# Two graph layers on one core: the first four graphs issued from a written-out opening with held loads

## The chip, the core and the metric

The kernel runs on one core of a Trainium2 chip. TensorE (PE) multiplies and transposes, VectorE (DVE), ScalarE (ACT) and GpSimd (POOL) work elementwise, and SyncE (SP) issues most DMAs. Each engine takes its instructions in order; engines wait for one another, and for DMAs, through semaphores. The metric is device time in microseconds of one execution; lower is better.

## The reference

64 graphs of 256 nodes with 256 features, all float32. Layer 0 normalises rows, aggregates over the degree-normalised adjacency and applies a weight. Layer 1 normalises again and combines a 17-tap convolution over the nodes, message passing over distances in a 3-dimensional embedding, and a GRU-like gate.

```
# layer 0
h   = relu(layernorm(x));  A = adj + I;  d = rowsum(A) ** -0.5   (0 where the sum isn't positive)
x   = x + relu((d * A * d) @ h @ W.T + b)
# layer 1
h   = relu(layernorm(x))
c   = relu(bn2(conv17(relu(bn1(conv1(h))))) + h)
s   = h @ w_se.T + b_se;  E = exp(-|s_n - s_m|^2)
m   = E @ relu(h @ w_msg.T + b_msg)
gi  = [c, m] @ w_ih.T + b_ih;  gh = h @ w_hh.T + b_hh
r, z = sigmoid(gi_r + gh_r), sigmoid(gi_z + gh_z)
out = x + (1 - z) * tanh(gi_n + r * gh_n) + z * h
```

## The kernel before, in words

One stage covers layer 0 and the first part of layer 1 for all 64 graphs, a loop over n = 0 to 68 (B + 5 passes). A second stage does the convolution's spectra and products and the gates. Graphs are loaded in pairs (G = 2), and a graph is two blocks of 128 rows (NB = 2). In pass n, PE works on graph n for layer 0 and on graphs n - 2, n - 4 and n - 5 for layer 1.

For each graph, layer 0 is this chain:

- `load` (lines 816 to 826) or, for the first pair, `load_one` (828): x and the adjacency come in.
- DVE takes row moments (`row_moments`, 832) and row sums (`degrees`, 844); POOL raises them to the power -1/2 (`factors`, 862); ACT writes the scaled, normalised rows `hs` (`layer0_in`, 876).
- PE transposes the adjacency (`turn_adj`, 891), ACT copies it out as `adjT`, POOL adds the unit matrix to make `adjH`, which has two buffers.
- PE multiplies (`aggregate`, 910: `ag`), ACT copies out `aggT`, PE multiplies by the weight (`project`, 925: `o`), and DVE makes the new rows x2 and their moments. POOL makes scales, and ACT writes the normalised rows `h2` (`norm`). DVE and ACT also empty PSUM banks; there are five general ones.

Layer 1's first part then turns h2 (`turn_h`, 984: `ht`), and multiplies it for the messages (`messages`, 1032: `ms`) and the 1-tap convolution (`conv1`, 1021: `c`). The weights are turned on PE as well (`turn_part`, `turn_away`), and the parts of w_ih and w_hh are written back turned. The batch-norm vectors go through `small_turns` (PE `t_bn`), `small_norms` (DVE and POOL, up to `sc`, `sh` and the diagonal `dg`), and `small_shift` (PE `t_b1`, which reads `dg`). The tap weights come by `TL` (`taps_load`, 643), a DMA of 2.2 MB issued by POOL, and are scaled by ACT.

The order around the change is written by hand. A `Pinned` wrapper (line 94) makes every instruction of an engine keep its place in the program's order among its engine's others. PE, ACT, DVE and POOL compute through such wrappers, so their lines are all the wrapper's, L102. DMAs issued as `nc.sync.dma_start` or `nc.scalar.dma_start` aren't pinned, and a planner places them. Work that follows PE's is deferred: `after(k, go)` puts it on a list, and every `beat` lowers all counts by one and issues what has fallen below zero. So `after(2, go)` issues at the third beat that follows.

In the kernel before, the first two graphs are loaded one by one and graphs 2 and 3 as a pair. The small vectors are issued by ACT's queue (`small_loads`, 697), and the loop starts at n = 0 with extra steps for n = 0 and n = 1 at the end of a pass.

Of the kernel before, what the change touches and what calls it, by code (L numbers as in the profile page):

```python
# [11 lines left out]
FP = mybir.dt.float32  # L12
# [173 lines left out]
def gnn_kernel(  # L186
# [9 lines left out]
    nc = tc.nc  # L196
# [14 lines left out]
    def scratch(name, shape):  # L211
# [26 lines left out]

    pe, act, vec, pool = (
        Pinned(tc, e) for e in (nc.tensor, nc.scalar, nc.vector, nc.gpsimd)
    )
    due = []
    paced = Paced(pool, vec, act)
# [1 line left out]
    def after(beats, go):  # L247
        due.append([beats, go])
# [296 lines left out]
    with ExitStack() as one:  # L545
# [11 lines left out]
        def beat(us):  # L557
            come_due()
            paced.issue(*(k * us for k in share))
# [36 lines left out]

        def load_part(src, o0, i, tag):
            nat = prep.tile([P, 2, i], FP, tag=f"nat{i}", name=f"nat_{tag}_{o0}", bufs=2)
            nc.sync.dma_start(
                nat, src[o0 * P : (o0 + 2) * P].rearrange("(c p) i -> p c i", p=P)  # L600
            )
            return nat
# [73 lines left out]
        def gate_biases_load():  # L676
            bi = prep.tile([P, 2 * D], FP, tag="bi", name="bi")
            bh = prep.tile([P, 2 * D], FP, tag="bh", name="bh")
            nc.sync.dma_start(bi, b_ih[0 : 2 * D].partition_broadcast(P))
            nc.sync.dma_start(bh, b_hh[0 : 2 * D].partition_broadcast(P))  # L680
            nc.sync.dma_start(bnB[:, 0:D], b_ih[2 * D : 3 * D].partition_broadcast(P))
            nc.sync.dma_start(bnB[:, D:], b_hh[2 * D : 3 * D].partition_broadcast(P))
            nc.sync.dma_start(dft, nc.inline_tensor(dft_table(), name="dft_c").ap())
            hold["b"] = bi, bh

        def gate_biases():
# [7 lines left out]
        ones = prep.tile([P, P], FP, tag="ones", name="ones")  # L694
        dg = prep.tile([P, DC, P], FP, tag="dg", name="dg")

        def small_loads():
            for k, v in enumerate((bn1_g, bn2_g, bn1_b, bn2_b, bn1_m, bn2_m, bn1_v, bn2_v)):
                nc.scalar.dma_start(
                    rows[DC * k : DC * (k + 1), :], v.rearrange("(c p) -> c p", p=P)  # L700
                )
            nc.scalar.dma_start(wsn, w_se)
            nc.scalar.dma_start(bmB[:, 0, 0:D], b_msg.partition_broadcast(P))
            nc.scalar.dma_start(bmB[:, 0, D : D + 3], b_se.partition_broadcast(P))
            nc.gpsimd.memset(ones, 1.0)

        def small_turns():

# [107 lines left out]
        def load(g):  # L816

            xt = io.tile([P, NR, D], FP, tag="x", name=f"x_{g}", bufs=3)
            at = io.tile([P, NR, N], FP, tag="adj", name=f"adj_{g}", bufs=3)
            st[g].update(both=(xt, at))  # L820
            for b in range(G):
                rb = slice(b * NB, (b + 1) * NB)
                st[g + b].update(xt=xt[:, rb, :], at=at[:, rb, :])
            if g > 0:
                nc.sync.dma_start(xt, x[g : g + G].rearrange("b (c p) d -> p (b c) d", p=P))
                nc.sync.dma_start(at, adj[g : g + G].rearrange("b (c p) d -> p (b c) d", p=P))

        def load_one(b):
            nc.sync.dma_start(st[b]["at"], adj[b].rearrange("(c p) d -> p c d", p=P))
            nc.sync.dma_start(st[b]["xt"], x[b].rearrange("(c p) d -> p c d", p=P))  # L830

        def row_moments(g, rows):
            xt, _ = st[g]["both"]
# [7 lines left out]
        def pairs(t):  # L841
            return t.rearrange("p (k r) -> p k r", k=2)

        def degrees(g, rows=range(NR)):

            _, at = st[g]["both"]
            mv = st[g]["mv"]
            if rows[0] == 0:
                for key in ("base", "pn"):
                    st[g][key] = small.tile(  # L850
                        [P, 2 * NR], FP, tag=key, name=f"{key}_{g}", bufs=1
                    )
                st[g]["deg"] = small.tile([P, NR], FP, tag="deg", name=f"deg_{g}", bufs=1)
            rs = slice(rows[0], rows[-1] + 1)
            deg, base, pn = st[g]["deg"][:, rs], pairs(st[g]["base"]), pairs(st[g]["pn"])
            vec.tensor_reduce(deg, at[:, rs, :], AX.X, ALU.add)
            vec.tensor_scalar(base[:, 0, rs], deg, 1.0, TINY, ALU.add, ALU.max)
            vec.tensor_scalar(base[:, 1, rs], mv[:, rs, 1], EPS, None, ALU.add)
            vec.tensor_scalar(pn[:, 0, rs], deg, 1.0, 0.0, ALU.add, ALU.is_gt)
            vec.tensor_scalar(pn[:, 1, rs], mv[:, rs, 0], -1.0, None, ALU.mult)  # L860
# [27 lines left out]
                    bias=nmr[:, r : r + 1], scale=rsd[:, r : r + 1],  # L888
                )

        def turn_adj(g):
            s = st[g]
            t = bank(f"at_{g}").rearrange("p (c i) -> p c i", c=NB)
            for jc in range(NB):
                for ic in range(NB):
                    pe.transpose(
                        t[:, jc, ic * P : (ic + 1) * P], s["at"][:, ic, jc * P : (jc + 1) * P], ident
                    )

            def keep():  # L900
                s["adjT"] = work.tile([P, NB, N], FP, tag="adjT", name=f"adjT_{g}", bufs=6)
                act.copy(s["adjT"], t)

            def hat():
                s["adjH"] = work.tile([P, NB, N], FP, tag="adjH", name=f"adjH_{g}")
                pool.tensor_tensor(s["adjH"], s["adjT"], eye, ALU.add)
            after(1, keep)
            after(2, hat)

        def aggregate(g):  # L910
            s = st[g]
# [205 lines left out]


        load(0)
        load_one(0)  # L1120
        nat_w0 = load_part(w0, 0, D, "w0")
        nc.sync.dma_start(b0B, b0.partition_broadcast(P))
        load_one(1)
        nat_wm = load_part(w_msg, 0, D, "wm")
        small_loads()
        load(G)
        L(WI, 0)()
        L(WI, 2)()

        full = eye.rearrange("p c d -> p (c d)")  # L1130
        t = ps_own.tile([P, NB, 512], FP, tag="ms", name="first_ms")
        for nb in range(NB):
            pe.matmul(t[:, nb, :], ident, full, start=True, stop=True)
        t = ps_own.tile([P, NB, D], FP, tag="c1", name="first_c1")
        pe.matmul(t, ident, full, start=True, stop=True)
        row_moments(0, range(NB))
        degrees(0, range(NB))
        factors(0, range(NB))
        turn_adj(0)
        beat(0.4)  # L1140
        layer0_in(0, range(NB))
        turn_part(w0T, nat_w0, 0, D, "w0")
        nat_w1 = load_part(conv1_w.rearrange("o i k -> o (i k)"), 0, D, "w1")
        row_moments(0, range(NB, NR))
        degrees(0, range(NB, NR))
        beat(0.4)
        factors(0, range(NB, NR))
        after(2, lambda: layer0_in(0, range(NB, NR)))
        after(3, lambda: row_moments(G, range(NR)))

        cv.bank, cv.beat = bank, beat
        items = []
# [35 lines left out]

        FILTER, SPECTRA, PRODUCTS = 2, 7, 4
        filtering = []  # L1190
        for n in range(B + 5):
            even, odd = n % G == 0, n % G == 1
            if filtering and not items:
                filtering.clear()
# [2 lines left out]
                conv_start()  # L1197
            if even and n + 2 * G < B:
                load(n + 2 * G)
            if 2 <= n <= B + 1:  # L1200
                turn_h(n - 2)
            beat(0.4)
            item()
            if n < B:
                aggregate(n)
                if odd and n + 1 < B and n > 0:
                    after(2, lambda n=n: factors(n + 1))
                    for r in range(NR):
                        after((5, 7, 8, 9)[r], lambda r=r, n=n: layer0_in(n + 1, (r,)))
                if even and 0 < n < B - G:  # L1210
                    for r in (0, 2):
                        after(1 + r // 2, lambda r=r, n=n: row_moments(n + G, (r, r + 1)))
                if even and n + G < B:
                    after(4, lambda n=n: degrees(n + G))
            beat(1.7)
            item()
            if even and 4 <= n <= B + 2:
                turn_cols(n - 4)
            beat(0.2)
            if n + 1 < B:  # L1220
# [4 lines left out]
                pass_messages(n - 5)  # L1225
            beat(1.7)
            item(True)
            if 2 <= n <= B + 1:
                messages(n - 2)
            beat(1.7)  # L1230
            item()
            if even and 4 <= n <= B + 2:
                distance(n - 4)
            beat(0.6)
            item()
# [1 line left out]
                project(n)  # L1237
            beat(1.7)
            item(True)
            if 2 <= n <= B:  # L1240
                conv1(n - 2)
            elif n == B + 2:
                conv1(B - 1)
            beat(1.7)
            item()
            if n == 0:
                small_turns()
                turn_part(wmT, nat_wm, 0, D, "wm")
                T(WI, 0)()
                L(WI, 4)()  # L1250
                own_bank("ms", 0, bmB)
            if n == 1:
                small_shift()
                turn_part(w1T, nat_w1, 0, D, "w1", scale=sc[:, 0:DC])
                beat(0.4)
                own_bank("c1", 0, b1B)
                T(WI, 2)()
                L(WH, 0)()
            if n >= 2 and later:
                for go in later.pop(0):  # L1260
                    go()
                if not later:
# [329 lines left out]
```

## Time and profile before

| | |
|---|---|
| Time before, median of 3 | 2079.03 us (2078.04 to 2083.53) |
| The profiled execution's own time | 2078.45 us |
| Its span | 2076.7 us |
| Granted PE clock over the span | 0.997 |
| PE busy in 0 to 10, 10 to 20, 20 to 30 us | 5.26, 8.32, 6.21 us |
| PE busy in 40 to 50 us | 10.00 us |
| DMA moved in 10 to 20, 20 to 30 us | 326, 352 GB/s |

A timeline line gives start, busy time, engine, source line, operation, output and inputs, shape and count. What stands in brackets is the engine's idle time just before, and what ended it. A window line gives busy time and count for PE, PE's weight loads, DVE, ACT and POOL, then the granted clock, the share of the DMA engines' time and GB/s. A matmul in float32 counts as two instructions.

### The profile page before, as it was taken

Reading aid. Unit: us, or ns where it says so; the run is one execution under the profiler, and the core shown is the slowest. Engines: PE = TensorE matmul, PEld = TensorE weight load, DVE = VectorE, ACT = ScalarE, POOL = GpSimd, SP = SyncE. Lnnn points to the kernel's source line nnn. Section 1 sums busy time; section 2 is a strip of 40 time slices with the busy share of each in tenths; the row PEclk is TensorE's granted clock in tenths of the full one; section 3 lists DMA queues with packets and bytes.
Section 4 is the critical chain, followed back from the end, with each engine's and each line's share of the span. In section 5 each row is a group of like instructions: output and inputs, shape, how many; then the busy total and the mean of one; then the engine's idle time right before and its main releaser. Section 6 shows DMA issues by size and latency. Waiting matters only on the chain. (4 is left out here: it accounts for less than half of the span.)

```text
span 2076.7 us, 31189 instructions
## 1 busy us (share of the span) xinstructions
PE 2028.5 (98%) x9977; PEld 1727.0 (83%) x9977; DVE 1404.7 (68%) x3181; ACT 997.5 (48%) x2165; POOL 1108.9 (53%) x1313
## 2 busy tenths in 40 slices
PE   7999999999999999899999999999999999999998
PEld 6877777888888787788888888888888888888887
DVE  6656666544688887337889815989924989965444
ACT  5756666665457676522344532234442234443333
POOL 4343333334775665347667527766726767644433
PEclk9999999999999999999999999999999999999999
DMA  9697987657765554656333455533346424322231
GB/s 307 241 255 245 264 252 251 208 178 228 242 203 195 178 178 148 202 178 203 122 117 117 138 177 187 167 102 117 126 154 195 155 92 127 117 87 89 95 97 61
DMA packets 292456, 352.84 MB, mean 170 GB/s; under 512 B 19491, under 2 KB 232118, under 8 KB 291638
## 3 DMA queue, kind: packets, MB, share of 16 engines
q1 hardware_dynamic: 291680, 346.26, 52.5%
q0 software_dynamic: 288, 4.46, 0.6%
q8 instruction: 80, 1.31, 0.3%
q14 instruction: 82, 0.67, 0.1%
q10 hardware_dynamic: 326, 0.14, 0.0%
HBM read 224.43 MB, written 126.35 MB: 169 GB/s over the span
## 5 line engine op out<-in xcount | busy, mean ns | idle before, releaser
L102 DVE SCALAR_TENSOR_TENSOR Xf<-Xf 128x256 f32<-128x256 f32 (+1 forms) x248 | 185.7, 763 | 6.1 <-ACT Xf L102 5.1
L102 DVE TENSOR_TENSOR Xf<-y,k 128x256 f32<-128x256 f32 x184 | 69.0, 416 | 178.3 <-PE y L102 175.3
L102 PE MATMUL ta<-T,S 128*128 128x256 f32 x768 | 186.6, 379 | 0.0
L102 PE MATMUL y<-wf,Xf 128*128 128x256 f32 x768 | 182.4, 380 | 2.5 <-DVE Xf L102 1.4
L102 POOL TENSOR_TENSOR rz<-u,p 128x256 f32<-128x256 f32 x64 | 48.0, 749 | 244.6 <-ACT u L102 244.6
L102 POOL TENSOR_TENSOR rs<-ve,mhalf 128x2 f32<-128x2 f32 (+1 forms) x65 | 52.2, 803 | 226.8 <-DVE nm L102 221.6
L102 ACT ACTIVATE rz<-rz 128x512 f32<-128x512 f32 x128 | 80.2, 627 | 180.6 <-DVE rz L102 180.6
L102 PEld LDWEIGHTS y<-wf,Xf 128*128 128x128 f32 x768 | 144.0, 190 | 24.9 <-DVE Xf L102 2.6
L102 PEld LDWEIGHTS ta<-T,S 128*128 128x128 f32 x768 | 145.9, 190 | 19.8
L102 PE MATMUL n<-wiT,hx 128*128 128x256 f32 x512 | 152.3, 379 | 0.0
L102 POOL TENSOR_TENSOR xs<-Xf 128x256 f32<-128x256 f32 x92 | 69.9, 766 | 133.9 <-PE y L102 72.7
L102 DVE SCALAR_TENSOR_TENSOR h2l<-rz,h2l 128x256 f32<-128x256 f32 x128 | 102.8, 803 | 53.6 <-POOL h2l L102 53.6
L102 POOL TENSOR_TENSOR aT<-e,adjT 128x512 f32<-128x512 f32 x64 | 85.8, 1358 | 94.1 <-ACT e L102 94.1
L102 PE MATMUL n<-whT,hx 128*128 128x256 f32 x512 | 131.4, 379 | 0.0
L102 PE MATMUL n<-wiT,xcT 128*128 128x256 f32 x512 | 131.4, 379 | 0.0
L102 PE MATMUL o<-w0T,aggT 128*128 128x256 f32 x512 | 125.6, 388 | 5.7 <-ACT aggT L102 4.1
L102 PE MATMUL ag<-adjH,hs 128*128 128x256 f32 x512 | 123.0, 382 | 7.5 <-POOL adjH L102 6.1
L102 PE MATMUL nm<-aT,mso 128*128 128x256 f32 x512 | 123.0, 384 | 7.1 <-POOL aT L102 4.5
L102 PE MATMUL ms<-wmT,h2T 128*128 128x259 f32 x512 | 124.3, 385 | 1.5 <-DVE h2T L102 1.5
L102 POOL TENSOR_TENSOR adjH<-adjT,eye 128x512 f32<-128x512 f32 x64 | 83.6, 1306 | 76.8 <-ACT adjT L102 76.8
L102 PE MATMUL c<-w1T,h2T 128*128 128x256 f32 x512 | 122.8, 383 | 0.0
L102 PEld LDWEIGHTS o<-w0T,aggT 128*128 128x128 f32 x512 | 95.3, 191 | 28.7 <-issue 5.6
(183 smaller groups left out, 5253.1 us busy)
## 6 DMA issues: line engine op xcount, KB each, us to landing
wf<-wfd SPq DMA_DIRECT2D x284, 256.0 KB
wfd<-fo SPq DMA_DIRECT2D x32, 576.0 KB
x2d<-x SPq DMA_DIRECT2D x64, 256.0 KB
h2d<-h SPq DMA_DIRECT2D x64, 256.0 KB
hTd<-h2T SPq DMA_DIRECT2D x64, 256.0 KB
h1d<-c1o SPq DMA_DIRECT2D x64, 256.0 KB
xnd<-xnT SPq DMA_DIRECT2D x64, 256.0 KB
h1l<-h1d SPq DMA_DIRECT2D x64, 256.0 KB
```

What stands on the lines that cost most here:

```text
L102: return self.tc.keep_in_program_order(getattr(self.engine, op)(*args, **kwargs))
```

## The change

A fifth wrapper, `sp`, pins most of SP's loads to the program's order. Graphs 0 to 3 are loaded one by one (`load_one`, adjacency first), with the first weight between graphs 0 and 1. The eleven small loads move from ACT's queue to SP's, behind the first part of w_ih. A one-column `warm` activation stands first on ACT. The warm-up matmuls on PE shrink to three, each on 32 rows. `degrees` takes the row sums ahead of the row moments, and `turn_adj` takes its beats and the engine of the unit-matrix sum as arguments; graph 1's sum goes to DVE. Passes 0 to 3 are replaced by `begin()`, which writes out their steps in another order: layer 0 of the four graphs stands in front, the weight turns and layer 1 of graphs 0 and 1 follow. The loop starts at n = 4.

```diff
-    pe, act, vec, pool = (
-        Pinned(tc, e) for e in (nc.tensor, nc.scalar, nc.vector, nc.gpsimd)
+    pe, act, vec, pool, sp = (
+        Pinned(tc, e) for e in (nc.tensor, nc.scalar, nc.vector, nc.gpsimd, nc.sync)
...
+        nc.gpsimd.memset(ones, 1.0)
+
         def small_loads():
...
-                nc.scalar.dma_start(
+                sp.dma_start(
                     rows[DC * k : DC * (k + 1), :], v.rearrange("(c p) -> c p", p=P)
                 )
...
-            if g > 0:
+            if g > G:
                 nc.sync.dma_start(xt, x[g : g + G].rearrange("b (c p) d -> p (b c) d", p=P))
...
-        def degrees(g, rows=range(NR)):
+        def degrees(g, rows=range(NR), stats=lambda: None):
...
             vec.tensor_reduce(deg, at[:, rs, :], AX.X, ALU.add)
+            stats()
+            mv = st[g]["mv"]
...
-        def turn_adj(g):
+        def turn_adj(g, at=(1, 2), by=pool):
...
-                pool.tensor_tensor(s["adjH"], s["adjT"], eye, ALU.add)
-            after(1, keep)
-            after(2, hat)
+                by.tensor_tensor(s["adjH"], s["adjT"], eye, ALU.add)
+            after(at[0], keep)
+            if at[1] is None:
+                return hat
+            after(at[1], hat)
...
         load(0)
+        load(G)
         load_one(0)
         nat_w0 = load_part(w0, 0, D, "w0")
-        nc.sync.dma_start(b0B, b0.partition_broadcast(P))
-        load_one(1)
+        for b in range(1, 2 * G):
+            load_one(b)
+        sp.dma_start(b0B, b0.partition_broadcast(P))
         nat_wm = load_part(w_msg, 0, D, "wm")
+        L(WI, 0)()
         small_loads()
-        load(G)
-        L(WI, 0)()
+        nat_w1 = load_part(conv1_w.rearrange("o i k -> o (i k)"), 0, D, "w1")
         L(WI, 2)()
 
+        warm = prep.tile([P, 1], FP, tag="warm", name="warm")
+        act.activation(warm, mhalf[:, 0:1], AF.Relu)
+
...
+        own_ms = ps_own.tile([P, NB, 512], FP, tag="ms", name="first_ms")
+        own_c1 = ps_own.tile([P, NB, D], FP, tag="c1", name="first_c1")
+        for r, t in enumerate((own_ms[:, 0, :], own_ms[:, 1, :], own_c1)):
+            at = slice(32 * r, 32 * (r + 1))
+            pe.matmul(t, ident[at, :], full[at, :], start=True, stop=True)
+
+        def stats(b):
+            g, rows = b // G * G, range(b % G * NB, (b % G + 1) * NB)
+            degrees(g, rows, lambda: row_moments(g, rows))
...
+        def begin():
+            stats(0)
+            turn_adj(0, (0, 0))
+            beat(0.4)
+            scale_rows(0)
+            turn_part(w0T, nat_w0, 0, D, "w0")
+            hat = turn_adj(1, (0, None), vec)
+            beat(0.4)
+            stats(1)
+            hat()
+            scale_rows(1)
+            rows_in(0)
+            turn_adj(2, (0, 0))
+            beat(0.4)
+            stats(2)
+            rows_in(1)
+            aggregate(0)
+            beat(1.7)
+            turn_adj(3, (0, 1))
+            scale_rows(2)
+            beat(0.4)
+            stats(3)
+            rows_in(2)
+            turn_part(wmT, nat_wm, 0, D, "wm")
+            aggregate(1)
+            load(2 * G)
+            scale_rows(3)
+            beat(1.7)
+            project(0)
+            beat(1.7)
+            rows_in(3)
+            T(WI, 0)()
+            L(WI, 4)()
+            aggregate(2)
+            beat(1.7)
+            project(1)
+            beat(1.7)
+            small_turns()
+            beat(0.1)
+            aggregate(3)
+            beat(1.7)
+            turn_adj(4)
+            own_bank("ms", 0, bmB)
+            beat(0.4)
+            row_moments(2 * G, range(NR))
+            degrees(2 * G)
+            project(2)
+            beat(1.7)
+            turn_h(0)
+            small_shift()
+            factors(2 * G)
+            beat(0.4)
+            turn_part(w1T, nat_w1, 0, D, "w1", scale=sc[:, 0:DC])
+            own_bank("c1", 0, b1B)
+            load(3 * G)
+            messages(0)
+            beat(1.7)
+            project(3)
+            beat(1.7)
+            conv1(0)
+            beat(1.7)
+            layer0_in(2 * G, range(2))
+            turn_h(1)
+            beat(0.4)
+            T(WI, 2)()
+            L(WH, 0)()
+            for k in range(2):
+                for go in later.pop(0):
+                    go()
+            layer0_in(2 * G, range(2, NR))
+            messages(1)
+            beat(1.7)
+            conv1(1)
+            beat(1.7)
...
-        for n in range(B + 5):
+        begin()
+        for n in range(4, B + 5):
```

The steps for n = 0 and n = 1 and the conditions on small n leave the loop with it.

More of the change, by code (lines that the diff above doesn't have):

```diff
@@ L598, in load_part @@
             nat = prep.tile([P, 2, i], FP, tag=f"nat{i}", name=f"nat_{tag}_{o0}", bufs=2)
-            nc.sync.dma_start(
+            sp.dma_start(
                 nat, src[o0 * P : (o0 + 2) * P].rearrange("(c p) i -> p c i", p=P)
@@ L678, in gate_biases_load @@
             bh = prep.tile([P, 2 * D], FP, tag="bh", name="bh")
[L679 to L683, printed above, removed]
+            sp.dma_start(bi, b_ih[0 : 2 * D].partition_broadcast(P))
+            sp.dma_start(bh, b_hh[0 : 2 * D].partition_broadcast(P))
+            sp.dma_start(bnB[:, 0:D], b_ih[2 * D : 3 * D].partition_broadcast(P))
+            sp.dma_start(bnB[:, D:], b_hh[2 * D : 3 * D].partition_broadcast(P))
+            sp.dma_start(dft, nc.inline_tensor(dft_table(), name="dft_c").ap())
             hold["b"] = bi, bh
@@ L695, in gnn_kernel @@
         dg = prep.tile([P, DC, P], FP, tag="dg", name="dg")
+        nc.gpsimd.memset(ones, 1.0)
         def small_loads():
             for k, v in enumerate((bn1_g, bn2_g, bn1_b, bn2_b, bn1_m, bn2_m, bn1_v, bn2_v)):
-                nc.scalar.dma_start(
+                sp.dma_start(
                     rows[DC * k : DC * (k + 1), :], v.rearrange("(c p) -> c p", p=P)
                 )
[L702 to L705, printed above, removed]
+            sp.dma_start(wsn, w_se)
+            sp.dma_start(bmB[:, 0, 0:D], b_msg.partition_broadcast(P))
+            sp.dma_start(bmB[:, 0, D : D + 3], b_se.partition_broadcast(P))
         def small_turns():
@@ L828, in load_one @@
         def load_one(b):
-            nc.sync.dma_start(st[b]["at"], adj[b].rearrange("(c p) d -> p c d", p=P))
-            nc.sync.dma_start(st[b]["xt"], x[b].rearrange("(c p) d -> p c d", p=P))
+            sp.dma_start(st[b]["at"], adj[b].rearrange("(c p) d -> p c d", p=P))
+            sp.dma_start(st[b]["xt"], x[b].rearrange("(c p) d -> p c d", p=P))
         def row_moments(g, rows):
@@ L842, in pairs @@
             return t.rearrange("p (k r) -> p k r", k=2)
-        def degrees(g, rows=range(NR)):
+        def degrees(g, rows=range(NR), stats=lambda: None):
             _, at = st[g]["both"]
-            mv = st[g]["mv"]
             if rows[0] == 0:
@@ L1130, in gnn_kernel @@
+        act.activation(warm, mhalf[:, 0:1], AF.Relu)
         full = eye.rearrange("p c d -> p (c d)")
[L1131 to L1149, printed above, removed]
+        own_ms = ps_own.tile([P, NB, 512], FP, tag="ms", name="first_ms")
+        own_c1 = ps_own.tile([P, NB, D], FP, tag="c1", name="first_c1")
@@ new lines, in gnn_kernel, with scale_rows, rows_in @@
+        for r, t in enumerate((own_ms[:, 0, :], own_ms[:, 1, :], own_c1)):
[4 more added lines that the diff above has]
+            degrees(g, rows, lambda: row_moments(g, rows))
+        def scale_rows(b):
+            factors(b // G * G, range(b % G * NB, (b % G + 1) * NB))
+        def rows_in(b):
+            layer0_in(b // G * G, range(b % G * NB, (b % G + 1) * NB))
@@ L1199, in gnn_kernel @@
                 load(n + 2 * G)
-            if 2 <= n <= B + 1:
+            if n <= B + 1:
                 turn_h(n - 2)
@@ L1205, in gnn_kernel @@
                 aggregate(n)
-                if odd and n + 1 < B and n > 0:
+                if odd and n + 1 < B:
                     after(2, lambda n=n: factors(n + 1))
@@ L1209, in gnn_kernel @@
                         after((5, 7, 8, 9)[r], lambda r=r, n=n: layer0_in(n + 1, (r,)))
-                if even and 0 < n < B - G:
+                if even and n < B - G:
                     for r in (0, 2):
@@ L1216, in gnn_kernel @@
             item()
-            if even and 4 <= n <= B + 2:
+            if even and n <= B + 2:
                 turn_cols(n - 4)
@@ L1227, in gnn_kernel @@
             item(True)
-            if 2 <= n <= B + 1:
+            if n <= B + 1:
                 messages(n - 2)
@@ L1231, in gnn_kernel @@
             item()
-            if even and 4 <= n <= B + 2:
+            if even and n <= B + 2:
                 distance(n - 4)
@@ L1239, in gnn_kernel @@
             item(True)
-            if 2 <= n <= B:
+            if n <= B:
                 conv1(n - 2)
@@ L1245, in gnn_kernel @@
             item()
[L1246 to L1259, printed above, removed]
+            if later:
                 for go in later.pop(0):
```

## The prediction

> **What bounds the kernel now.** I read the page first (busy shares, 40 slices), then each engine's timeline over the first 75 us, one-microsecond windows there, and SP's waits.
>
> ```profile
> span 2076.7 us, 31189 instructions
> ...
> PE 2028.5 (98%) x9977; PEld 1727.0 (83%) x9977; DVE 1404.7 (68%) x3181; ACT 997.5 (48%) x2165; POOL 1108.9 (53%) x1313
> ...
> PE   7999999999999999899999999999999999999998
> ```
>
> PE is busy 98%, and idles 48 us in all. The change edits the first four graphs, so what it can win is what PE loses in the first slice (the 7). PE's timeline shows those losses and a landmark:
>
> ```profile
> 2.79 3.53 PE L102 MATMUL first_ms<-eye,ident 128*128 128x512 f32 x4 [2.79 <-POOL eye L568]
> ...
> 7.02 0.60 PE L102 MATMUL at<-ident,adj 128*128 128x128 f32 x4
> ...
> 11.38 2.46 PE L102 MATMUL ag<-adjH,hs 128*128 128x256 f32 x8 [3.32 <-POOL adjH L102]
> ...
> 25.38 2.80 PE L102 MATMUL o<-w0T,aggT 128*128 128x256 f32 x8 [3.79 <-ACT aggT L102]
> ...
> 47.97 0.60 PE L102 MATMUL ht<-ident,h 128*128 128x128 f32 x4
> ```
>
> The `ht` at 47.97 is `turn_h(2)`, the first work of n = 4. Before it lies the very set of PE work that `begin()` issues; from n = 4 the program is the same. So the change is worth 47.97 minus the time at which `turn_h(2)` starts afterwards. After each gap the granted clock (third number from the end) is halved:
>
> ```profile
> 13.00:14.00 1.00, 1.00 (x4) 0.71 (x4) 0.00 (x0) 0.62 (x2) 0.27 (x2) 0.50 1.09 378
> 27.00:28.00 1.00, 1.00 (x4) 0.72 (x4) 0.00 (x0) 1.00 (x3) 0.43 (x1) 0.50 1.08 383
> ```
>
> It has a price: from 25.38 to `ht` at 30.64 PE does 1.73 + 4 x 0.44 = 3.5 us of work (spacings of the same groups after 34 us: `o` 1.73, four transposes 0.44) in 5.3, so 1.8 is lost; the first gap likewise about 1.9. DVE, ACT, POOL and SP around it:
>
> ```profile
> 14.51 0.43 DVE L102 BATCH_NORM_STATS2 st<-x 128x6 f32<-128x256 f32 x1 [2.96 <-DMA x<-in_x_dram]
> ...
> 23.39 0.48 DVE L102 TENSOR_SCALAR dg<-ident,sh 128x128 f32<-128x128 f32 x2
> ```
> ```profile
> 7.13 1.28 ACT L102 ACT_TABLE_LOAD   x1 [7.13 <-DMA rows<-in_L_gnn_bn_v_dram]
> ```
> ```profile
> 36.20 0.76 POOL L102 DMA_DIRECT2D w2n<-in_L_gnn_conv_w_dram  x1
> ...
> 45.58 0.62 POOL L102 DMA_DIRECT2D w2n<-in_L_gnn_conv_w_dram  x1
> ```
> ```profile
> SPq L825 <- DMA adj<-in_adj_dram: 2.0, 1, 2.0
> ...
> SPq L829 <- DMA rows<-in_L_gnn_bn_g_dram: 0.9, 1, 0.9
> ```
>
> DVE waited in order for graph 2's rows until 14.51, and the second PE gap hangs on that through moments(0), scales(0) and norm(0), which stands ahead of aggT(1) on ACT. ACT's table came late because eleven small DMAs stood on its queue. SP itself waited for small loads.
>
> **What the skill says.** "TensorE: Matmul & The Clock Gate", Part 1: an idle window of about 3.4 us drops PE to half rate, and sustained work of that length restores it; the 0.50 after gaps of 3.32 and 3.79 agrees. Part 3 of that page: matmuls on different 32-row groups run together; here the four `di` matmuls of K = 5 take 0.71 against 1.89 for four full ones of equal width. "ScalarE: Activation LUTs", What ACT_TABLE_LOAD costs: 1.28 us; the trace has 1.28. "DMA: Bandwidth & Descriptors", Issuing engines are not separate DMA queues: moving an issue to another engine saves only sequencer time; the trace shows 350 to 385 GB/s for 12 to 29 us whoever issued.
>
> **The change part by part** (durations from the trace of before).
>
> *Warm-up.* Three matmuls of 512 columns on three row groups instead of three in sequence. In sequence they end near 7.0; together I take two cold passes of 0.9, so 2.79 + 1.8 + 0.3 = 4.9. PE is then not warm, so at(0) takes 0.9 and not 0.44.
>
> *ACT table and small loads.* The warm activation puts the 1.28 us at about 2 to 3.3; the eleven issues leave ACT. Worth nothing alone: ACT waits for at(0) until 5.9. On SP the small loads add 11 x 0.45 = 5 us after WI 0, until about 12 to 13. `rows` is wanted by t_bn at 22, `bmB` at 24, so hidden; uncovered, they would cost PE their delay one for one.
>
> *Loads.* Nine of 256 KB ahead at 365 GB/s is 0.7 us each: graph 3 complete by about 10 (first x usable at 4.41 before, issued 1.25). Graph 4/5's 1 MB is due by 20; DVE wants it at 26.6, so hidden by 6 us. SP's own order is now held: WI 4 waits there for WI 0's turn (about 19.5), the second w_hh part for t_w1 (about 32), and the stores x2d, hTd and graph 6's load can stand behind them; graph 6 is wanted near 50 and a store has a second buffer, so I cost this at nothing, up to 1 if a store comes late.
>
> *Start.* at(0) 4.9 to 5.9; adjT(0) on ACT 0.57; adjH(0) on POOL 1.27; factors(0), now behind it, 1.88; two hs 1.09; five hand-overs of 0.06: ag(0) at 11.0, against 11.38. So the front end wins 0.4 only: POOL in series replaces PE and the table. And ag(0) is cold, 1.9 more. adjH(1) on DVE costs DVE 0.8 (its 128x512 sums elsewhere), and takes 1.27 from POOL; DVE has done all four graphs' statistics (4 x 2.1 + 0.6 + 0.8 from 3.8) by 14 and then idles, so neither counts. The `ones` fill (0.20 on POOL) moves within start-up, before POOL has work.
>
> *PE dense.* ag0 1.73, at3 0.44, wm 0.44, ag1 1.73, o0 1.73, WI0 0.88, ag2 1.73, o1 1.73 = 10.4; with 1.9: o(1) ends at 23.3 (before 28.0). adjH has two buffers, so adjH(2) waits for ag(0) and adjH(3) for ag(1), with factors(2), (3) behind them on POOL; hs(2) is ready about 2 us before ag(2), so covered. This is the gain, 4.7 us.
>
> *New wait.* `small_norms` defers its second half by three beats, and so `sc`, `sh`, `dg` are issued on DVE behind moments and degrees of graphs 4 and 5. DVE from rows(1): rows 1.72, bn 0.42, moments(1) 1.33, four row moments 2.16, degrees 1.61, sc to dg 1.1 = 8.3, so dg at 31.8. PE has t_bn 0.28, ag3 1.73, at4 0.44, o2 1.73, ht0 0.44 = 4.6 and then stands at t_b1 from 27.9: 4.0 us idle, cold again. Behind t_b1 in PE's order are t_w1, ms0, o3, c0. ms0 wants h2T(0): rows(2) 1.72, b1B 0.33, moments(2) 1.33, copy 0.68 = 4.1 more, 35.9; PE idles another 2.7.
>
> *Rest.* From ms0: 1.76, o3 1.73, c0 1.73, ht1 0.44, WI 2 and 4 1.76, ms1 1.76, c1 1.73 = 10.9, and 1.5 of the clock: 48.3. The same hand arithmetic on the old order gives 49.0 where the trace has 47.97; it runs 1.0 late, and I take off 0.7: 47.6.
>
> *Collisions and taps.* dg and x2 rows on DVE can overlap POOL's pow (bounds 0 and 1.5; the x2 row took 1.53 at 56.05 beside POOL's mask, 0.42 elsewhere): 0.4. TL(0) now stands on POOL behind scales(3), about 45 instead of 36.20. Before, it landed 10.4 to 11.4 us after issue: 56, where ACT wants it at 56.4. ACT is full from 57.5 to 69.3 (11.77 of 11.80), aggT there leads `o` by 0.9. Bounds 0 and 3; I take 0.4.
>
> Sum: 47.6 + 0.4 + 0.4 - 47.97 = +0.4. The profiled execution took 2078.45, 1.75 of it outside its span: 2078.9. The median is 0.58 above that execution: 2079.4. Own range of this case 2076 to 2083.
>
> **Rivals.**
> *Stalls don't bind (faster).* If DVE reached dg by 27.9, both stalls and their clock fall away: 4.0 + 2.7 + 1.7 = 8.4, so 2071. For it: before, dg took 1.1 us after its scale. Against: DVE needs 8.3 us in order after o(1), and I find no gap there to cut; even o(1) 2 us earlier (PE warm at ag0) gives only 2077.
> *Taps late (slower).* If the two 2.2 MB loads, now issued within 1 us of each other, share the engines instead of following one another, both land near 45 + 21 = 66. Scaling at 56.4 then blocks ACT 9.6 us; past the 0.9 of slack PE stalls: 2079 + 8.7 = 2088. It decides once TL(0) lands 7 us after ACT wants it. For: nothing separates them; against: one queue.
> *Loads spread.* Up to eight loads in flight share bandwidth: graph 2's x(2), issued at 7.45, came 7 us later. If graph 0 and 1 come 2 us later, ag(0) slips about 1, and graph 4's data may reach DVE 2 late: 2081.5.
>
> **How the numbers follow.** A difference under 0.3% (6.2 us) is what I call the same. Forecast 0.60 (2079.4), loads spread 0.18 (2081.5), taps late 0.14 (2088), stalls don't bind 0.08 (2071). Faster 0.08 from the last; slower 0.14 from the taps; same 0.78. The range, 2074 to 2088, takes the first two whole and about half of the taps.
>
> **What would show it.** Right: ag(0) near 11 at clock 0.50 later; o(1) ending near 23; PE idle of about 4 us before t_b1 put down to DVE dg, about 2.7 before ms put down to h2T; turn_h(2) near 48; TL near 45. Wrong: no wait at t_b1, DVE waiting for x at 25 or later, or ACT idle before w2n.

## The result and the profile after

The changed kernel takes 2094.39 us (median of 6 runs, 2093.37 to 2097.79) against 2079.12 for the kernel before on the same chip. The ratio is 1.0073, with a 95% interval of 1.0063 to 1.0083: 15 us slower. The profiled execution took 2094.92 us with a span of 2093.1, which is 16.4 more than the span before. The page of the changed kernel, head and PE's 40 slices:

```profile
span 2093.1 us, 31218 instructions
...
PE 2035.6 (97%) x9977; PEld 1731.8 (83%) x9977; DVE 1408.7 (67%) x3187; ACT 998.1 (48%) x2166; POOL 1109.2 (53%) x1316
...
PE   7799999999999999899999999999999999999998
```

The first slice is as it was; the second has fallen from 9 to 7. PE's timeline over the first 90 us tells the rest (start, busy time, group, and in brackets the idle time before it and what ended it):

```profile
10.47 3.42 PE L102 MATMUL ag<-adjH,hs 128*128 128x256 f32 x8 [0.82 <-ACT hs L102]
...
20.65 1.89 PE L102 MATMUL o<-w0T,aggT 128*128 128x256 f32 x8
...
30.79 1.19 PE L102 MATMUL t_b<-dg,ones 128*128 128x128 f32 x4 [2.92 <-DVE dg L102]
...
34.98 3.82 PE L102 MATMUL ms<-wmT,h2T 128*128 128x259 f32 x8 [2.15 <-DVE h2T L102]
...
49.07 0.60 PE L102 MATMUL ht<-ident,h 128*128 128x128 f32 x4
49.50 1.89 PE L102 MATMUL ag<-adjH,hs 128*128 128x256 f32 x8
63.62 1.09 PE L102 MATMUL st<-ident,cols 128*128 128x128 f32 x4 [12.23 <-DVE cols L102]
...
69.15 1.99 PE L102 MATMUL o<-w0T,aggT 128*128 128x256 f32 x8
```

Two things stand here. The opening goes nearly as forecast, and gives back at t_b1 and ms what it had won by o(1): `turn_h(2)` comes at 49.07, 1.1 us later than before. And then PE stands still for 12.23 us in pass 4, in which the diff changes next to nothing. From `turn_h(2)` to project(4), the `o` behind it, PE took 5.5 us before, from 47.97 to this line of the kernel before:

```profile
53.50 1.99 PE L102 MATMUL o<-w0T,aggT 128*128 128x256 f32 x8
```

It takes 20.1 now (49.07 to 69.15). With 1.1 + 14.6 that is 15.7 of the 16.4 us.

Windows of 4 us show how complete the stop is. The columns are PE, its weight loads, DVE, ACT and POOL busy with counts, then clock, DMA share and GB/s:

```profile
54.00:58.00 4.00, 0.00 (x0) 0.00 (x0) 0.00 (x0) 0.00 (x0) 0.00 (x0) 0.54 0.98 415
58.00:62.00 4.00, 0.00 (x0) 0.00 (x0) 0.00 (x0) 0.00 (x0) 0.00 (x0) 0.50 0.97 348
62.00:66.00 4.00, 2.38 (x10) 2.31 (x11) 3.53 (x13) 2.83 (x6) 0.00 (x0) 0.50 0.96 335
```

From 54 to 62 every engine is idle and the DMA engines are full. PE comes back at half clock, which is in the 14.6. What ends the stop is in DVE's timeline (a copy from a PSUM bank into a tile is called an eviction here):

```profile
45.29 0.68 DVE L102 COPY w_wi<-t_wi 128x512 f32<-128x512 f32 x1
62.30 0.69 DVE L102 COPY w_wi<-t_wi 128x512 f32<-128x512 f32 x1 [16.33 <-DMA wid<-w_wi]
```

The second line is the eviction of the second half of w_ih's last part, `T(WI, 4)`, and it waits for a store. DVE takes its instructions in order, so `cols`, which PE's transpose at 63.62 reads, stood behind it. `turn_away` evicts into tiles of tag `away`, which has two buffers. `begin()` issues `T(WI, 2)` and `T(WI, 4)` one behind the other, four evictions in a row, so the third and fourth need the buffers of the first and second back, and these are free only when their stores to `wid` have landed. Those stores (`wid<-w_wi`) were issued here on SP's timeline, and both loads of tap weights, called tap loads below, here on POOL's:

```profile
45.82 0.95 SPq L639 DMA_DIRECT2D wid<-w_wi  x2
46.82 1.24 SPq L102 DMA_DIRECT2D nat_wh<-in_L_gnn_w_hh_dram  x2
```
```profile
45.70 1.31 POOL L102 DMA_DIRECT2D w2n<-in_L_gnn_conv_w_dram  x2
```

The two entries of `later` that `begin()` pops there put TL(0) between the two turns and TL(1) right behind the second, so both tap loads go out in 1.3 us, 4.46 MB. In the kernel before they stood 9.4 us apart, and the two turns about 17 us; DVE's evictions of them came there without a wait:

```profile
32.21 0.68 DVE L102 COPY w_wi<-t_wi 128x512 f32<-128x512 f32 x1
...
48.63 0.69 DVE L102 COPY w_wi<-t_wi 128x512 f32<-128x512 f32 x1
```

Now the first store landed (its data had arrived) within 3.4 us (ACT waited 3.8 for it), the second about 16 us after its issue, when the second tap load did. The DMA view of 44 to 64 us gives for each queue its packets, MB and share of the 16 DMA engines' time, and for an issue its size and median time to landing. q0 is POOL's queue, q1 SP's:

```profile
q0 software_dynamic: 288, 4.46, 55.9%
q1 hardware_dynamic: 2676, 2.84, 42.9%
...
w2n<-in_L_gnn_conv_w_dram POOLq DMA_DIRECT2D x2, 2176.0 KB, 13.1
```

### The profile page after: what moved, and what is told of

The parts are those of the page before. It is cut to its first block, busy times and chain, and to the rows that moved or that the text cites. A ratio compares the mean times of both kernels' runs of the same rounds, so it can differ in the third digit from the quotient of the medians.

```text
span 2093.1 us, 31218 instructions
## 1 busy us (share of the span) xinstructions
PE 2035.6 (97%) x9977; PEld 1731.8 (83%) x9977; DVE 1408.7 (67%) x3187; ACT 998.1 (48%) x2166; POOL 1109.2 (53%) x1316
## 3 DMA queue, kind: packets, MB, share of 16 engines
q0 software_dynamic: 288, 4.46, 0.5%
## 5 line engine op out<-in xcount | busy, mean ns | idle before, releaser
L102 POOL TENSOR_TENSOR rs<-ve,mhalf 128x2 f32<-128x2 f32 x65 | 52.2, 802 | 227.3 <-DVE nm L102 225.3
L102 PEld LDWEIGHTS ms<-wmT,h2T 128*128 128x128 f32 x512 | 98.0, 194 | 30.2 <-issue 12.9
```

The source lines that it names most:

```text
L102: return self.tc.keep_in_program_order(getattr(self.engine, op)(*args, **kwargs))
```

## Experiments

Each ratio below is to runs of the kernel before taken beside that run's, with the 95% interval in brackets.

**Theory.** A transfer that SP issues beside or behind the two tap loads lands only when they do. It costs time where something due waits for it, and in the changed kernel that is the fourth eviction. **Rival 1:** the taps' traffic alone stops the core, whatever the buffers. **Rival 2:** two buffers are too few for four evictions in a row, taps or not.

**own_buffers: the last part's evictions in other tiles.**

```diff
-                    w = prep.tile([P, 2, 2 * P], FP, tag="away", name=f"w_{tag}_{i0}_{o0}", bufs=2)
+                    own = tag == "wi" and o0 == 4
+                    w = prep.tile(
+                        [P, 2, 2 * P], FP, tag=("bi", "bh")[i0 // 2] if own else "away",
+                        name=f"w_{tag}_{i0}_{o0}", bufs=1 if own else 2,
+                    )
```

> The changed kernel, with the two evictions of w_ih's last part put into tiles of their own (those that later hold two biases) instead of the two that hold the part before. Theory (the eviction waits for a store of its buffer, and that store crawls beside the two tap loads): DVE's wait of 16.3 us goes, turn_h(2) stays near 49, and with at most 4 us for the next store beside the taps the time is 2080 to 2084. Rival 1 (the two tap loads issued together stop the core by their traffic alone): the wait moves to another line and the time stays above 2090. Rival 2 (two buffers turned over at once are too few, taps or not): as the theory, 2080.

Measured 2088.04 us, ratio 1.0043 (1.0029 to 1.0057). DVE's wait is gone and `turn_h(2)` stands at 49.38. But PE stops later in pass 4, before the turn of w_hh's first part. PE's line, and SP's issue of that load (the profile is of the slowest of the five executions, 2093.07, the others took 2087.86 to 2090.60):

```profile
64.99 1.09 PE L102 MATMUL t_wh<-ident,nat_wh 128*128 128x128 f32 x4 [6.35 <-DMA nat_wh<-in_L_gnn_w_hh_dram]
```
```profile
47.15 1.23 SPq L102 DMA_DIRECT2D nat_wh<-in_L_gnn_w_hh_dram  x2
```

Issued 1.1 us after the first tap load, 256 KB took 17 to 18 us. So my 2080 to 2084 was wrong: the wait went to another line, as rival 1 said, though to under its 2090. Rival 2 had said 2080; alone it doesn't explain a load that waits, and taps_apart puts it to the test.

**own_buffers_wh_early: the next due transfer taken out of the way too.** The taps still go out together. On top of own_buffers:

```diff
             L(WI, 4)()
+            L(WH, 0)()
             aggregate(2)
...
             T(WI, 2)()
-            L(WH, 0)()
```

> As own_buffers (evictions of w_ih's last part in tiles of their own, both tap loads still together), and the first load of w_hh, which PE waited 6.4 us for there, issued about 20 us earlier on SP, behind w_ih's last part. Theory (the tap loads cost only what is issued beside or behind them and is due before they land, 16 to 18 us): no transfer due in that time is left, so 2080 to 2084. Rival (traffic alone costs): the wait moves on to a third line, 2087 or more.

Measured 2080.72, ratio 0.9999 (0.9990 to 1.0007): the whole loss is gone, with both tap loads still together. POOL's line and PE's next two `turn_h`, which stand 9.52 us apart, as in the kernel before (47.97 and 57.49):

```profile
45.82 1.31 POOL L102 DMA_DIRECT2D w2n<-in_L_gnn_conv_w_dram  x2
```
```profile
49.20 0.60 PE L102 MATMUL ht<-ident,h 128*128 128x128 f32 x4
...
58.72 0.60 PE L102 MATMUL ht<-ident,h 128*128 128x128 f32 x4
```

Rival 1 falls: the traffic is the same but for the one 256 KB load, and no loss is left to measure once nothing due lies in it.

**taps_apart: the other half of the cause taken away.** The two buffers stay.

```diff
-            [TL(0), L(WH, 2)],
-            [T(WI, 4), TL(1)],
-            [S(0, 0), S(0, 1), S(0, 2), S(0, 3), T(WH, 0), L(WH, 4)],
+            [L(WH, 2)],
+            [T(WI, 4)],
+            [TL(1), S(0, 0), S(0, 1), S(0, 2), S(0, 3), T(WH, 0), L(WH, 4)],
...
             factors(2 * G)
             beat(0.4)
+            TL(0)()
```

> The changed kernel, with the first tap load issued about 12 us earlier (behind graph 4's factors) and the second a pass later, the two buffers kept. Theory: the eviction waits for a store's ordinary trip, at most 3 us, 2080 to 2083. Rival 1 (traffic): 2080. Rival 2 (too few buffers whatever the traffic): the wait stays over 10 us, 2091 to 2095.

Measured 2082.48, ratio 1.0011 (1.0002 to 1.0019). The taps now go out at 34.65 and 59.81. The wait in the list of waits is:

```profile
DVE w_wi L102 <- DMA wid<-w_wi: 3.9, 1, 3.9
```

That is a store's trip with only ordinary traffic beside it, 3.9 us against 16.3 (I had said at most 3), and PE stands still for no more than 0.2 in that pass. Rival 2 falls: the same two buffers take four evictions in a row.

**second_tap_later: half the dose.** The first tap load stays where the change put it.

```diff
-            [T(WI, 4), TL(1)],
-            [S(0, 0), S(0, 1), S(0, 2), S(0, 3), T(WH, 0), L(WH, 4)],
+            [T(WI, 4)],
+            [TL(1), S(0, 0), S(0, 1), S(0, 2), S(0, 3), T(WH, 0), L(WH, 4)],
```

> The changed kernel, with only the second tap load moved a pass later; the first stays in front of the turn of w_ih's last part, the two buffers stay. Theory (a store issued beside the taps lands when they do): the second eviction buffer comes free near 56, when 2.2 MB are in, instead of 62; DVE's wait falls from 16.3 to 8 to 11 us and the time to 2086 to 2090. If the second load is what does the harm: 2080 to 2083. If any one tap load does all of it: 2093 or more.

Measured 2088.5, ratio 1.0042 (1.0027 to 1.0057), as the theory said, and in its list of waits:

```profile
DVE w_wi L102 <- DMA wid<-w_wi: 10.8, 1, 10.8
```

With no, one and two tap loads in flight, the same eviction waits 3.9, 10.8 and 16.3 us; PE stops for 0, 6.7 and 12.2.

**before_cause_put_in and before_taps_together: the cause in the old order.** The first puts the sequence into pass 3 of the kernel before:

```diff
-            [TL(0), L(WH, 2)],
-            [T(WI, 4), TL(1)],
+            [L(WH, 2)],
+            [T(WI, 2), TL(0), T(WI, 4), TL(1)],
...
-                T(WI, 2)()
```

The second puts only the taps there, and leaves `T(WI, 2)` at its place:

```diff
-            [TL(0), L(WH, 2)],
-            [T(WI, 4), TL(1)],
+            [L(WH, 2)],
+            [T(WI, 4), TL(0), TL(1)],
```

> The kernel before, with the changed kernel's sequence put in at the end of pass 3: turn of w_ih's middle part, first tap load, turn of its last part, second tap load. Theory: an eviction waits 10 us or more for a store, and the time is 2089 to 2096. Rival 1 (traffic): the same. Rival 2: the same. If none holds and the loss lies elsewhere in the opening: 2079 to 2083.

> The kernel before, with the first tap load moved 9.4 us later, next to the second, behind the turn of w_ih's last part. Theory: no eviction meets a store of its buffer there, so at most a little of ACT's scaling waits, 2079 to 2083. Rival 1 (traffic alone): 2090 or more. Rival 2: 2079.

The first took 2094.67 (1.0073, 1.0058 to 1.0088), the changed kernel's own ratio. The stop is in the same pass, from DVE's and PE's timelines:

```profile
62.67 0.69 DVE L102 COPY w_wi<-t_wi 128x512 f32<-128x512 f32 x1 [13.42 <-DMA wid<-w_wi]
```
```profile
62.60 1.12 PE L102 MATMUL at<-ident,adj 128*128 128x128 f32 x4 [11.06 <-ACT w_wi L102]
```

Here ACT's eviction (waiting 12.7 us) and DVE's were both held. The second took 2082.34 (1.0011, 1.0003 to 1.0020): taps together without the turns cost about 2 us, 4 at most, and no stop appears. A store issued at 49.47 beside those taps was out until 63, and ACT's next eviction into its buffer, a pass later, waited 0.8 us for it. So the cause needs none of the new opening. The rest of the change (held loads, small loads on SP, table first, shorter warm-up, layer 0 in front) comes out about even: own_buffers_wh_early keeps all of it and stands at 0.9999.

**apart_dg_early: the opening's first stall.** `finish` one beat earlier, on top of taps_apart.

```diff
-            after(2, finish)
+            after(1, finish)
```

> As taps_apart, and the diagonal dg of the batch-norm shift issued one beat earlier, ahead of graph 4's row moments on DVE. If DVE's order is what PE waits for: the wait at t_b1 (2.8 us) goes, but the wait of ms for h2T stays where DVE's queue puts it, at 35, and takes the time over: under 1 us gained, 2081 to 2083. If the wait at t_b1 counts for itself: 2079 or less.

Measured 2081.5 (1.0004, 0.9996 to 1.0012), not told apart from taps_apart. On DVE `dg` now comes at 26.68 instead of 30.44, and PE's wait at t_b1 has gone over to ms:

```profile
35.19 3.82 PE L102 MATMUL ms<-wmT,h2T 128*128 128x259 f32 x8 [5.91 <-DVE h2T L102]
```

DVE's order holds the opening, not either wait alone.

**mended, mended_warm, mended_further: a version that beats both.** mended joins taps_apart, own_buffers, the early w_hh load, the early `dg`, and

```diff
-                (act.copy if any(paced.lines) else vec.tensor_copy)(s["hT"], t)
+                (act.copy if g == 0 or any(paced.lines) else vec.tensor_copy)(s["hT"], t)
```

> taps_apart with own_buffers, the first w_hh load early, dg one beat earlier, and graph 0's h2T emptied by ACT, which idles there, instead of DVE. If the two waits in the opening are what holds turn_h(2) at 49: both go, with the half clock behind them, turn_h(2) at 41 to 43, and the time is 2072 to 2076. If DVE's total work holds it: 2079 or more.

Measured 2075.76, ratio 0.9978 (0.9969 to 0.9987). Both waits are gone and `turn_h(2)` stands at 45.38, not at 41 to 43, since conv1(0) now waits:

```profile
29.44 2.02 PE L102 MATMUL ms<-wmT,h2T 128*128 128x259 f32 x8
...
36.34 3.54 PE L102 MATMUL c<-w1T,h2T 128*128 128x256 f32 x8 [3.17 <-DVE cols L102]
...
45.38 0.60 PE L102 MATMUL ht<-ident,h 128*128 128x128 f32 x4
```

conv1(0) reads the weight w1T, and not `cols`. DVE empties w1T just ahead of `cols` (35.52 to 36.20), behind graph 4's moments and graph 2's rows.

mended gains 0.2%, about 4.6 us, with several steps at once; the runs don't split it among them.

mended_warm repeats the three 32-row warm-up matmuls behind the turn of adjacency 0.

> As mended, with three more 32-row matmuls on PE behind the turn of adjacency 0, as cover for the clock. If the ag(0) at half rate (3.42 us against 1.89) follows from too little PE work before it: ag(0) under 2.2 us and 1 us better than mended. If 32-row matmuls and transposes don't count: ag(0) as slow, and up to 1 us worse.

Measured 2075.19 (0.9974, 0.9963 to 0.9985), the same as mended within the intervals. ag(0) takes 2.56, not the 3.78 of mended, though not under the 2.2 I had said, and it starts at 11.00 instead of 10.46:

```profile
11.00 2.56 PE L102 MATMUL ag<-adjH,hs 128*128 128x256 f32 x8 [0.32 <-ACT hs L102]
```

mended_further also moves graph 4's statistics behind conv1(0), on top of mended_warm, and empties graph 1's h2T by ACT.

> As mended_warm, with graph 4's row moments, degrees and factors behind conv1(0) instead of ahead of project(2), its scaled rows behind them, and graph 1's h2T emptied by ACT too. If DVE's order is what holds conv1(0) in mended_warm (3.2 us and half clock behind it): turn_h(2) at 40.5 to 42.5 and 2071 to 2073.5. If the moved work comes late for aggregate(4): a new wait there and 2074 to 2077.

Measured 2075.36 (0.9982, 0.9975 to 0.9990), no better. Its profiled execution took 2081.14, 5.8 above its median. In it ag(4) waits 2.36 us, until 48.72: ACT writes its rows only from 48.04, behind the moved work, as the second branch had said. DVE's timeline shows waits of another kind, beside POOL's issue of the first tap load:

```profile
30.17 0.42 DVE L102 SCALAR_TENSOR_TENSOR x<-pre,x 128x256 f32<-128x256 f32 x1 [2.40 <-DMA x2d<-x]
...
39.24 0.42 DVE L102 SCALAR_TENSOR_TENSOR x<-pre,x 128x256 f32<-128x256 f32 x1 [4.56 <-DMA x2d<-x]
```
```profile
28.61 0.76 POOL L102 DMA_DIRECT2D w2n<-in_L_gnn_conv_w_dram  x1
```

The rows x2 have two buffers as well. The second wait, 34.67 to 39.24, ends within a microsecond of this tap load's landing (10 us after its issue) and fits the same mechanism in a third place. The first began at 27.77, before the tap load went out, so it has another cause, which stays open. One profile doesn't tell how often either happens.

## Why the prediction was wrong, by its steps

The forecast was 2079.4, with a range of 2074 to 2088; measured were 2094.39. The step that failed is the cost of stores and loads in flight, put at nothing ("Loads" below).

- **What bounds the kernel, and the landmark**: right. PE's losses in the opening decided until `turn_h(2)`. Wrong was "from n = 4 the program is the same, so the change is worth 47.97 minus" its start: the program is the same, but what is in flight when it starts is not. 14.6 of the 16.4 us lie behind the landmark.
- **Warm-up, table, start**: right in kind and size. ag(0) at 11.0 forecast, 10.47 measured, cold as said: 3.42 us against 1.89, though the granted clock reads 1.00 there, so only the durations tell. The small loads left SP at 15, not 12 to 13, still hidden.
- **The clock**: the prediction took half clock behind gaps of 3.32 and 3.79 as agreeing with the idle window that it cites. Here it also stood behind idle times of 2.92 (before t_b1) and 2.53 (before the last transposes of w_ih in mended_further), while behind 2.36 (before ag(4) there) it stayed at 1.00. Transposes stand just ahead of all three, so the runs don't tell whether PE's idle time alone counts.
- **PE dense**: o(1) ends at 22.5, forecast 23.3. The gain up to there was 5.6, forecast 4.7.
- **New wait**: right in place and cause, forecast about a third too long. t_b1 waited 2.92 for DVE (4.0 forecast), ms 2.15 for h2T (2.7), with half clock behind: ms took 3.82.
- **Rest**: `turn_h(2)` came at 49.07, and the sum had 48.3 before I took 0.7 off. That they lie near is partly luck: ms began at 34.98, 0.9 earlier than forecast, and the way from there took 14.1 us, not 12.4, chiefly because half clock cost ms and o(3) 2.9 us and not 1.5.
- **Loads**: graph 4's rows were in time for DVE (no wait at 26.06); PE waited 0.34 for its adjacency. But "a store has a second buffer, so I cost this at nothing, up to 1 if a store comes late" is the step that failed, together with the four turns of w_ih, counted in "Rest" as 1.76 us of PE and nothing else. The stores that it names are x2d and hTd; those of w_ih, which had the second buffer but needed it back at once, are not among them. I didn't ask how many buffers `turn_away` evicts into, nor what was issued with its stores. The cost was a wait of 16.3 us on DVE and of 12.2 on PE.
- **Collisions and taps**: the issue near 45 was right (45.70), and so was the first landing near 56 (10.3 us after issue). ACT's scaling, which I priced at 0 to 3, was not the victim.
- **Rival, taps late**: it had the two loads within 1 us of each other, and their joint landing as the price. They landed at 56 and 62.4, not both near 66. It named the wrong waiter: I looked for who waits for the taps, not for who waits for what goes out beside them. It said 2088; with the eviction it is 2094.
- **Rival, stalls don't bind**: not so in the changed kernel. Taking both stalls away on top of mended transfers (mended) gave 2075.8, about 4.6 us of the rival's 8.4, since a third DVE wait stood behind them.
- **Rival, loads spread**: neither of its signs came; PE waited 0.64 for graph 2's adjacency and 0.34 for graph 4's.

## What to carry to other kernels

When work is drawn together, list the DMAs that it issues as well as its instructions, and for each store ask which buffer it frees and when that buffer is wanted again; a pair of buffers covers four uses in a row only if its stores land quickly (3.9 us here against 16.3). In these runs a large load on one queue held up the transfers on another that were still on their way, so put it where nothing due follows for as long as it takes. A landmark behind which "nothing changes" holds only if queues, buffers and transfers in flight are the same there too.

## What the runs showed of the hardware that I had not expected

A 256 KB store issued within a microsecond of two 2.2 MB loads took about 16 us, and a 256 KB load right behind them 17 to 18, though they are on another queue and the two loads are only 4.46 MB. Ordinary traffic beside the store gave 3.9. The two queues shared by packets and not by bytes. In 44 to 64 us POOL's queue moved 4.46 MB in 288 packets, 15 KB each, and SP's 2.84 MB in 2676, 1.1 KB each. From 46 to 48, with the tap loads issued but none of their packets seen yet, SP's queue moved 539 packets alone, which is how the first store could land by 49.2:

```profile
q1 hardware_dynamic: 539, 0.65, 103.1%
```

From 50 to 60, with both at work, they moved nearly the same number of packets, 241 and 237, and so 3.90 MB and 0.24:

```profile
q0 software_dynamic: 241, 3.90, 93.9%
q1 hardware_dynamic: 237, 0.24, 6.9%
```

This agrees with the Trainium skill, "DMA: Bandwidth & Descriptors", Queues, rings and completion order, which says that an engine takes turns between queues packet by packet. It also gives the dose, by an estimate from these numbers: a 256 KB store in packets of about 1 KB needs some 256 turns, and two tap loads have 288 packets and one has 144. So the store is in when both loads are nearly in, and with one load soon after that is in. No run changed the packets' size, so that a smaller size would help is not shown. SP's own issues stretched beside the tap loads too: one store's took 8.00 us in before_taps_together, where most take 0.3 to 0.5.

The three 32-row matmuls (2.1 us) and the transposes behind them left PE at half rate for ag(0), 3.42 us against 1.89, although PE, once it had begun, was never idle for more than 0.82 us before it. Three more such matmuls shortened it to 2.56 in the profile of mended_warm and to 2.05 in that of mended_further.
